# Layer 0 routing of images 0 to 2 moved into the attention loop, with its lists on GpSimd

## The chip, the cores and the metric

The kernel runs on one core of a Trainium2 chip, as one launch. Its time is the device time in microseconds (us) of that launch; the median of ten runs of the kernel before is given below. A core has five engines that run side by side, each with its own in-order queue of instructions: PE (TensorE, matrix products and transposes), ACT (ScalarE), DVE (VectorE), POOL (GpSimd) and SP (SyncE, which here issues DMAs). An instruction waits for instructions of other engines through semaphores, and while it waits, everything behind it in its own queue waits too.

## The reference, cut to what matters

The network has two layers on four images of 256 channels and 32 x 32 = 1024 tokens.

```
x  = x + attention(layernorm(x))          # layer 0, top-k attention, 8 heads, a gate sets k
t  = layernorm(x) per token, no affine    # eps 1e-5
logits = t @ router_w.T                   # 8 experts
rw, re = top_k(softmax(logits), 2); rw = rw / sum(rw)
out = t + sum over the two experts of rw * (gelu(t @ w1[e] + b1[e]) @ w2[e] + b2[e])
# layer 1: layernorm, a selective scan in four directions, layernorm,
#          and an 8-expert top-2 MoE with a per-expert layernorm and 1024 hidden columns
```

"Routing" below means all that lies between the attention's output x and the moment that the token rows stand in the expert order in DRAM: the logits, the two best experts, the mean and the deviation of each token, the two weights, the place of each token in its expert's list, and the scatter of the token rows.

## The kernel before, in words

**Attention.** A work item of the attention is a *half* (one tile of 128 queries and one group of four heads); there are 64, 16 to an image (`PER`), in the order of the images. The loop `for i in range(len(order) + 8): turn(i)` runs 72 turns. A turn works on halves of four ages at once: `h0` (this turn's half: `take` at L655 copies its scores from PSUM to SBUF on ACT, then counts begin), `h1` and `h2` (counts and updates of a threshold, L621 on ACT and L625 on DVE), and `h3` (windows and the selection on DVE, L672 and L675, then four masks on POOL, L705, and six small `verify` operations on POOL, L694 to L699). Two halves make a `Pair`, whose weights (L760, L765), exponentials (L773) and sums (L783) run in the turns after. The order in which the engines get their instructions is the order in which `turn` writes them out; nothing reorders it afterwards. The line that is run first in a turn after `h0.scores(1)` is `h0.take(0)`.

**Work beside the attention.** `plan(first, needed, steps, places)` enters a generator into a list; `beside(i, place)` takes one step of the most urgent entry at each of five places of a turn (places 0 to 4); `due` forces what is needed. So are placed the queries and keys of the next head group, the values, `rest` (the depthwise convolution, L548 to L581), and `finish` (the projection and the residual, L601 and L604), which writes the final x of image b in turns 16b + 20 to 16b + 23.

**Layer 0 routing.** Class `Routing0` handles an image in two generators. `norm` computes the logits on PE (L216), copies them on DVE, transposes the image on PE into token rows (L226), copies these on ACT (L228) into a buffer of their own (`token_rows`, one of the ring `s`), and gets the sum of squared deviations by Square on ACT (L231). `route` finds the deviation by a bit trick and three Newton steps on DVE (L256 to L261), normalises the rows on ACT (L264), picks the two experts on DVE (L270 to L281), takes the exponential for the weights on ACT (L282), counts with two matrix products (L284, L285), and places the tokens on DVE (L288 to L302). The last call also makes the table of the expert tiles. All four images are planned behind the last half: `norm` from turn 64 and turn 69 on, `route` from turn 67 and turn 70 on. After the loop, 64 indirect DMAs on POOL (L240, 16 for an image, all in one group without dependencies on each other) scatter the rows into `slots_x0`.

**Layer 0 MoE.** 36 tiles (`USUAL`) of 256 rows each; `Tile0` loads rows (L1704) and weights (L1707, L1709) on SP, transposes the rows (L1715), runs two products with a Gelu between them (L1739), multiplies by the weight on ACT (L1752), adds the residual on DVE (L1753), and stores the rows by a DMA on POOL. Behind it come the scan of layer 1 and the second MoE.

**Storage.** x of each image is a tile [128, 2, 1024] (channels in the partitions). `zeros` is a constant tile from which DMAs in turn 3 (into `slots_x`) and turn 20 (into `slots_x0`) fill two DRAM arrays.

Of the kernel before, what the change touches and what calls it, by code (L numbers as in the profile page):

```python
# [21 lines left out]
P = 128  # L22
B = 4
# [23 lines left out]
W0 = C + 3  # L47
# [15 lines left out]
def metaformer(ctx: ExitStack, tc: tile.TileContext, t: dict, out: bass.AP):  # L63
# [12 lines left out]
    x = [cons.tile([P, CT, L], F32, tag=f"x{b}", name=f"x{b}") for b in range(B)]  # L76
# [13 lines left out]
    def layer_norm_steps(dst, src, eps, room, psum, tag):  # L90

        sq = room("ln_sq")
        for h in range(NHALF):
            cols = ts(h, HALF)
            mean = psum.tile([P, HALF], F32, tag=tag, name="ln_mean")
            for c in range(CT):
                nc.tensor.matmul(mean, mean_w, src[:, c, cols], start=(c == 0), stop=(c == CT - 1))
            for c in range(CT):
                nc.vector.tensor_tensor(dst[:, c, cols], src[:, c, cols], mean, ALU.subtract)
                nc.scalar.activation(sq[:, c, cols], dst[:, c, cols], AF.Square)  # L100
# [16 lines left out]
        for h in range(NHALF):  # L117
            rb = psum.tile([P, HALF], F32, tag=tag, name="ln_rb")
            for i in range(HALF // P):
                n = h * (HALF // P) + i  # L120
                nc.tensor.matmul(rb[:, ts(i, P)], rs[:, n : n + 1].to_broadcast([P, P]), ident,
                                 start=True, stop=True)
            for c in range(CT):
                nc.vector.tensor_tensor(dst[:, c, ts(h, HALF)], dst[:, c, ts(h, HALF)], rb, ALU.mult)

    def layer_norm(dst, src, eps, pool, psum, tag):
        for _ in layer_norm_steps(dst, src, eps, lambda n: pool.tile([P, CT, L] if n == "ln_sq" else [P, NT], F32,
# [10 lines left out]
    zeros = cons.tile([P, W0], F32, tag="zeros", name="zeros")  # L138
    nc.vector.memset(zeros, 0.0)
    nc.gpsimd.iota(zeros[:, C : C + 1], [[0, 1]], base=2 * B * L, channel_multiplier=2,  # L140
                   allow_small_or_imprecise_dtypes=True)
# [11 lines left out]
    base0 = cons.tile([P, E], F32, tag="base0", name="base0")  # L153
# [10 lines left out]
    nc.gpsimd.iota(place, [[0, 1]], base=0, channel_multiplier=1, allow_small_or_imprecise_dtypes=True)  # L164
    tiles0 = cons.tile([P, PHASES, E], F32, tag="tiles0", name="tiles0")
# [23 lines left out]

    class Routing0:  # L190

        def __init__(self, space, rest, bank, group):
            self.bank, self.group, self.rest = bank, group, rest
            room = carved(space)
            self.before = room([P])
            nc.gpsimd.memset(self.before, 1.0)
            nc.gpsimd.affine_select(out=self.before, in_=self.before, pattern=[[1, P]], compare_op=ALU.is_gt,
                                    fill=0.0, base=0, channel_multiplier=-1)
            self.keep = room([E, NT])
            nc.vector.memset(self.keep, 1.0)  # L200
            nc.vector.memset(self.keep[:, :, 0:1], 0.0)
            nc.vector.tensor_copy(base0, region)
            self.small = [[room([NT]) for _ in range(2)] for _ in range(B)]
            self.logits = [room([NT, E + 1]) for _ in range(B)]

        def norm(self, b, rows, ready=(True, True)):

            ve, nm = self.small[b]
            for h in range(NHALF):
                while not ready[h]:  # L210
                    yield None
                four = slice(4 * h, 4 * h + 4)
                raw = self.bank("raw")[:, : 4 * (E + 1)].rearrange("p (n e) -> p n e", e=E + 1)
                for i in range(4):
                    for c in range(CT):
                        nc.tensor.matmul(raw[:, i], x[b][:, c, ts(4 * h + i, P)], rw0[:, c, :],  # L216
                                         start=(c == 0), stop=(c == CT - 1))
                yield True
                nc.vector.tensor_copy(self.logits[b][:, four], raw)
                nc.vector.tensor_scalar(nm[:, four], raw[:, :, E], -C ** -0.5, None, ALU.mult)  # L220
                yield False
                for r in (2 * h, 2 * h + 1):
                    tp = self.bank("tp").rearrange("p (i c) -> p i c", c=C)
                    for i in range(2):
                        for c in range(CT):
                            nc.tensor.transpose(tp[:, i, ts(c, P)], x[b][:, c, ts(2 * r + i, P)], ident)  # L226
                    yield True
                    nc.scalar.copy(rows[:, ts(r, 2), :C], tp)  # L228
                    for i in range(2):
                        n = 2 * r + i  # L230
                        nc.scalar.activation(tp[:, i], tp[:, i], AF.Square, bias=nm[:, n : n + 1], scale=C ** -0.5,  # L231
                                             accum_out=ve[:, n : n + 1])
                    yield False

        def send(self, b, rows):

            here = sent[:, :, ts(b, NT)]
            for n in range(NT):
                for k in range(2):
                    ins = nc.gpsimd.indirect_dma_start(  # L240
                        out=slots_x0, out_offset=bass.IndirectOffsetOnAxis(ap=here[:, k, n : n + 1], axis=0),
                        in_=rows[:, n], in_offset=None).ins
                    tc.declare_no_dep(ins, group=self.group, reason="rows of their own")
                    tc.add_to_no_dep_group(self.group, ins)

        def route(self, b, rows):

            here = sent[:, :, ts(b, NT)]
            room = carved(self.rest)
            wide = [P, NT, E]  # L250
            ve, nm = self.small[b]
            lg, eq, hot1, hot2, both, place_, pick = (room([NT, E]) for _ in range(7))
            tote, cum = room([E, NT]), room([E, NT])
            rr, r0, rs, red, m1, m2 = (room([NT]) for _ in range(6))
            place_ = flat(place_).rearrange("p (e n) -> p e n", n=NT)
            nc.vector.tensor_scalar(ve, ve, 1e-5, None, ALU.add)  # L256
            nc.vector.tensor_scalar(r0.bitcast(I32), ve.bitcast(I32), -0.5, RSQRT_BITS, ALU.mult, ALU.add)
            for src, dst in ((r0, rs), (rs, r0), (r0, ve)):
                nc.vector.tensor_tensor(rr, src, src, ALU.mult)
                nc.vector.scalar_tensor_tensor(rr, rr, -0.5, ve, ALU.mult, ALU.mult)  # L260
                nc.vector.scalar_tensor_tensor(dst, rr, 1.5, src, ALU.add, ALU.mult)  # L261
            nc.vector.scalar_tensor_tensor(nm, nm, C ** 0.5, ve, ALU.mult, ALU.mult)
            for n in range(NT):
                nc.scalar.activation(rows[:, n, :C], rows[:, n, :C], AF.Identity, bias=nm[:, n : n + 1],  # L264
                                     scale=ve[:, n : n + 1])
            nc.vector.tensor_tensor(lg, self.logits[b][:, :, :E], ve.unsqueeze(2).to_broadcast(wide), ALU.mult)
            yield None

            def best(value, hot):
                nc.vector.tensor_reduce(value, lg, AX.X, ALU.max)  # L270
                nc.vector.tensor_tensor(eq, lg, value.unsqueeze(2).to_broadcast(wide), ALU.is_equal)
                nc.vector.tensor_tensor(eq, eq, first.unsqueeze(1).to_broadcast(wide), ALU.mult)
                nc.vector.tensor_reduce(red, eq, AX.X, ALU.max)
                nc.vector.tensor_tensor(hot, eq, red.unsqueeze(2).to_broadcast(wide), ALU.is_equal)

            best(m1, hot1)
            nc.vector.tensor_scalar(rows[:, :, C], red, -1.0, float(E), ALU.mult, ALU.add)
            nc.vector.scalar_tensor_tensor(lg, hot1, -1e30, lg, ALU.mult, ALU.add)
            best(m2, hot2)
            nc.vector.tensor_tensor(both, hot1, hot2, ALU.add)  # L280
            nc.vector.tensor_tensor(m2, m2, m1, ALU.subtract)  # L281
            nc.scalar.activation(m2, m2, AF.Exp)  # L282
            sums = self.bank("sums")[:, : 2 * NT * E].rearrange("p (k f) -> p k f", k=2)
            nc.tensor.matmul(sums[:, 0], self.before, flat(both), start=True, stop=True)  # L284
            nc.tensor.matmul(sums[:, 1], mean_w, flat(both), start=True, stop=True)  # L285
            yield True
            sums = sums.rearrange("p k (n e) -> p k n e", e=E)
            nc.vector.tensor_scalar(tote, sums[:, 1].rearrange("p n e -> p e n"), float(C), None, ALU.mult)  # L288
# [1928 lines left out]
```

## Time and profile before

| what | us |
|---|---|
| median of 10 runs | 4078.67 |
| lowest and highest of them | 4070.32, 4088.41 |
| the profiled execution | 4079.1 |
| its span (first to last instruction) | 4077.4 |
| mean granted TensorE clock of the span | 0.877 |
| attention turns 0 to 63 | 113.6 to 1819.6 |
| turns 24, 25, 26, 27, 28 begin | 737.4, 764.9, 790.6, 818.5, 847.9 |
| first and last scatter of layer 0 (L240) | 1914.5, 1994.8 |
| first load of an expert tile (L1704) | 2002.25 |
| first transpose of the layer 0 MoE (L1715) | 2009.1 |

All times of instructions are counted from the span's start, in the one profiled execution. A row of the timeline gives the start, the duration, the engine, the line of the code, the operation, what it writes and reads, and in square brackets how long the engine had been idle before it and what ended that. In a row of the groups, the column behind the bar is busy time and the mean duration of one in nanoseconds, and then the idle time in front of the group. In the page's part 2 the span is cut into 40 slices of 102 us, and a digit is the busy share of a slice in tenths; the attention fills slices 2 to 18, and slice 20 (1937 to 2039 us) holds the scatters.

### The profile page before, as it was taken

Reading aid. Unit: us, or ns where it says so; the run is one execution under the profiler, and the core shown is the slowest. Engines: PE = TensorE matmul, PEld = TensorE weight load, DVE = VectorE, ACT = ScalarE, POOL = GpSimd, SP = SyncE. Lnnn points to the kernel's source line nnn. Section 1 sums busy time; section 2 is a strip of 40 time slices with the busy share of each in tenths; the row PEclk is TensorE's granted clock in tenths of the full one; section 3 lists DMA queues with packets and bytes.
Section 4 is the critical chain, followed back from the end, with each engine's and each line's share of the span. In section 5 each row is a group of like instructions: output and inputs, shape, how many; then the busy total and the mean of one; then the engine's idle time right before and its main releaser. Section 6 shows DMA issues by size and latency. Waiting matters only on the chain. (4 is left out here: it accounts for less than half of the span.)

```text
span 4077.4 us, 50231 instructions
## 1 busy us (share of the span) xinstructions
PE 3519.6 (86%) x17474; PEld 1951.2 (48%) x17474; DVE 3022.7 (74%) x5391; ACT 2833.8 (70%) x3793; POOL 1786.8 (44%) x1437
## 2 busy tenths in 40 slices
PE   8378888788788878877498999999999999999996
PEld 5134434434343434334275434444444434788885
DVE  2689898989998898896366899899899899411112
ACT  2889999999999998995135666767767677422222
POOL 0145444554554444655434656445445446121111
PEclk8567788788878877787699999999999999999997
DMA  9400094000000000000475434334324334655565
GB/s 288 101 1 1 1 237 111 1 1 19 1 1 1 11 1 1 1 11 22 144 227 163 117 107 133 104 100 126 116 97 127 108 103 139 192 184 187 187 193 191
DMA packets 241817, 393.34 MB, mean 96 GB/s; under 512 B 31888, under 2 KB 182160, under 8 KB 241424
## 3 DMA queue, kind: packets, MB, share of 16 engines
q1 hardware_dynamic: 218992, 340.51, 27.9%
q0 software_dynamic: 19904, 48.42, 3.6%
q8 instruction: 141, 2.31, 0.2%
q10 hardware_dynamic: 2656, 1.09, 0.1%
q14 instruction: 124, 1.02, 0.1%
HBM read 280.34 MB, written 109.61 MB: 96 GB/s over the span
## 5 line engine op out<-in xcount | busy, mean ns | idle before, releaser
L705 POOL TENSOR_SCALAR dr<-s_n,last 128x1024 bf16<-128x1024 f32 x256 | 731.4, 2875 | 881.2 <-DVE state L733 425.6
L621 ACT ACTIVATE junk_a<-s_n,state 128x1024 int8<-128x1024 f32 x448 | 514.5, 1149 | 25.1 <-DVE state L739 6.9
L1889 POOL TENSOR_TENSOR da_c<-prod,come 128x1024 f32<-128x1024 f32 x128 | 247.7, 1935 | 436.1 <-DVE h L1895 385.5
L625 DVE TENSOR_SCALAR_CACHE_REDUCE junk_v<-s_n,state 128x1024 int8<-128x1024 f32 x320 | 408.6, 1277 | 8.8
L2065 ACT ACTIVATE hid<-hp,b 128x256 f32<-128x256 f32 x288 | 133.7, 474 | 355.5 <-PE hp L2063 355.3
L672 DVE SCALAR_TENSOR_TENSOR w<-s_n,win 128x1024 f32<-128x1024 f32 x256 | 347.4, 1357 | 5.3
L675 DVE MAX8 win<-w 128x8 f32<-128x1024 f32 x256 | 314.5, 1228 | 8.8
L1856 POOL TENSOR_TENSOR uu<-dx,bb 128x1024 f32<-128x1024 f32 x127 | 302.3, 2381 | 1.6 <-DMA bb<-bc_d 1.6
L621 ACT ACTIVATE junk_a<-s_n,guess 128x1024 int8<-128x1024 f32 x256 | 294.0, 1149 | 7.4
L773 ACT ACTIVATE ex<-sT 128x1024 f32<-128x1024 f32 x256 | 247.0, 1015 | 66.0 <-PE sT L765 65.8
L1895 DVE TENSOR_TENSOR_SCAN h<-da_c,uu 128x1024 f32<-128x1024 f32 x127 | 288.6, 2272 | 0.0
L1869 DVE TENSOR_TENSOR_SCAN h<-da,uu 128x1024 f32<-128x1024 f32 x127 | 288.4, 2271 | 0.0
L1878 DVE TENSOR_TENSOR_SCAN h<-da,uu 128x1024 f32<-128x1024 f32 x127 | 287.3, 2262 | 0.0
L783 PE MATMUL o_ps<-ex,vT 128*32 128x256 f32 x2048 | 240.2, 455 | 39.2 <-ACT ex L773 32.7
L655 ACT COPY s_n<-sp 128x1024 f32<-128x1024 f32 x256 | 256.7, 1003 | 23.3 <-PE sp L647 10.8
L1840 ACT ACTIVATE da_c<-delta,a_log 128x1024 f32<-128x1024 f32 x128 | 268.6, 2098 | 5.9 <-issue 5.8
L1899 PE MATMUL hp<-h,ident 128*128 128x512 f32 x512 | 250.8, 613 | 22.8 <-DVE h L1895 22.6
L2063 PE MATMUL hp<-xe,w 128*128 128x256 f32 x1152 | 258.6, 381 | 6.3 <-DVE xe L2051 6.1
L2074 DVE TENSOR_TENSOR ys<-yp,b2e 128x512 f32<-128x512 f32 x36 | 24.9, 692 | 320.2 <-PE yp L2071 320.2
L2071 PE MATMUL yp<-w2e,hid 128*128 128x256 f32 x1152 | 255.9, 379 | 0.0
L1864 PE MATMUL hp<-da_c,ident 128*128 128x512 f32 x512 | 248.0, 607 | 6.4 <-POOL da_c L1889 3.7
L1857 ACT COPY uu<-uu 128x1024 f32<-128x1024 f32 x127 | 252.0, 1985 | 1.7 <-POOL uu L1856 1.7
(598 smaller groups left out, 7438.3 us busy)
## 6 DMA issues: line engine op xcount, KB each, us to landing
cb<-bc_d SPq DMA_DIRECT2D x128, 512.0 KB, 4.1
bb<-bc_d SPq DMA_DIRECT2D x127, 512.0 KB, 5.0
w<-in_w SPq DMA_DIRECT2D x36, 1024.0 KB, 5.3
w2e<-in_w SPq DMA_DIRECT2D x36, 1024.0 KB, 5.6
slots_x<-zeros SPq DMA_DIRECT2D x1, 33411.0 KB, 133.9
slots_x<-zeros SPq DMA_DIRECT2D x1, 33282.0 KB, 129.4
w<-in_w SPq DMA_DIRECT2D x72, 256.0 KB, 3.4
xs<-slots_x SPq DMA_DIRECT2D x36, 259.0 KB, 3.5
```

Source lines behind the costliest of these rows:

```text
L621: nc.scalar.activation(junk, self.row(r), AF.Sign, bias=thr, scale=-1.0, accum_out=u)
L625: nc.vector.tensor_scalar(junk, self.row(r), thr, None, ALU.is_lt, ALU.add, accum_out=u)
L655: nc.scalar.copy(self.s[e][:, :, ts(h, HALF)], self.sp[h][e])
L672: nc.vector.scalar_tensor_tensor(w, self.row(r), self.win[:, r, 0:1], self.row(r), ALU.is_gt if r < LAST_DVE else ALU.is_ge, ALU.subtract, ...
L675: nc.vector.max(out=self.win[:, r, 1:], in_=w)
L705: ins = nc.gpsimd.tensor_scalar(dr, self.row(r), self.last[:, r : r + 1], None, ALU.is_lt)
L1840: nc.scalar.activation(grid(self.da_c), cols_flipped(self.prep.delta[:, self.c]), AF.Exp, scale=self.decay)
L1856: nc.gpsimd.tensor_tensor(self.uu[:, 0], self.prep.dx[:, self.c], self.bb, ALU.mult)
L1869: nc.vector.tensor_tensor_scan(rows.rearrange("p r w -> p (r w)"), self.da, self.uu[:, 0], 0.0, ALU.mult, ALU.add)
L1878: nc.vector.tensor_tensor_scan(hs[:, ::-1], self.da[:, ::-1], self.uu[:, 0][:, ::-1], 0.0, ALU.mult, ALU.add)
L1895: nc.vector.tensor_tensor_scan(hs, self.da_c, self.uu[:, 1], 0.0, ALU.mult, ALU.add)
L2063: nc.tensor.matmul(hp[:, f % 2], self.w1[:, c, ts(f, P)], self.xe[:, c], start=(c == 0), stop=(c == CT - 1))
```

## The change

- x is kept in a wider tile `store` of 8 rows of `W0` = 261 columns; while layer 0 runs, it is read as `xr[b][:, n, :]`, 128 tokens n by 256 channels, with five spare columns (before three). `block(b, c, h)` is the view that the layer norm, queries and keys, values, `rest` and `finish` use in place of the slice of x.
- For images 0 to 2 the routing is planned in the attention itself, from turn0 = 16b + 24 on (24, 40 and 56). `feed` (PE logits, DVE choice of two experts, transposes on PE, ACT copies into x's own place) is planned from place 0 of turn0 - 1; `count` from place 3 of turn0 + 1.
- The deviation is computed on POOL, in the new calls `behind_masks`, which stand behind the masks and `verify` of the turn: `spread` for tiles 0 to 3 in turn0 + 1, `spread` for tiles 4 to 7 and `root` in turn0 + 2; `locate` in turn0 + 3; and two scatters in each of the turns turn0 + 5 to turn0 + 12, now not in a group without dependencies.
- The exponential of the weights is in `share`, called by `before_masks` right behind `h0.take(0)` of turn0 + 3. `shares` (two operations on DVE) is in turn0 + 3, `fix` (DVE) in turn0 + 4.
- Image 3 is routed in two halves (`halved`), planned from turns 68 and 70; its 16 scatters follow the loop. `table` is a function of its own.
- Rows are scattered as they are, not normalised. `Tile0.normed` normalises them on ACT (two activations of 128 x 256 for a tile) before the transposes; `small` gets two more DVE operations, and in `store` the multiplication is an activation with a bias of the same size.
- The two DMA fills change places (turn 3 and turn 20); the ring `s` is sized 2 x 1024 again; the second layer's residual operation on DVE that added op to x becomes a copy; `before` and `bases` are shared by the layers.

The core of the diff:

```diff
+        for b in range(B - 1):
+            turn0 = b * PER + 24
+            routings[turn0] = Routing0(b, bank, lambda: scratch("space0"))
+            plan((turn0 - 1) * PLACES, turn0 + 1, routings[turn0].feed())
+            plan((turn0 + 1) * PLACES + 3, turn0 + 3, routings[turn0].count())
+
+        def behind_masks(i):
+            for turn0, routing in routings.items():
+                at = i - turn0
+                if at == 1:
+                    routing.spread((0, 1))
+                if at == 2:
+                    routing.spread((2, 3))
+                    routing.root()
+                if at == 3:
+                    routing.shares()
+                    routing.locate()
+                if at == 4:
+                    routing.fix()
+                if 5 <= at < 13:
+                    send(routing.b, (at - 5,), None)
+
+        def before_masks(i):
+            for turn0, routing in routings.items():
+                if i - turn0 == 3:
+                    routing.share()
...
             if h0:
                 h0.scores(1)
                 h0.take(0)
+            before_masks(i)
             beside(i, 0)
...
                 h3.verify()
...
+            behind_masks(i)
             beside(i, 3)
```

The new POOL work and the exponential:

```diff
+        def spread(self, pairs):
+            for r in pairs:
+                nc.gpsimd.tensor_tensor(self.squares, xr[self.b][:, ts(r, 2), :C],
+                                        self.mean[:, ts(r, 2)].unsqueeze(2).to_broadcast([P, 2, C]), ALU.subtract)
+                nc.gpsimd.tensor_tensor(self.squares, self.squares, self.squares, ALU.mult)
+                half = C // 2
+                while half > 1:
+                    nc.gpsimd.tensor_tensor(self.squares[:, :, :half], self.squares[:, :, :half],
+                                            self.squares[:, :, half : 2 * half], ALU.add)
+                    half //= 2
+                nc.gpsimd.tensor_tensor(self.ve[:, ts(r, 2)], self.squares[:, :, 0], self.squares[:, :, 1], ALU.add)
+
+        def root(self):
+            nc.gpsimd.tensor_scalar(self.ve, self.ve, 1.0 / C, 1e-5, ALU.mult, ALU.add)
+            nc.gpsimd.tensor_tensor(self.rs, self.ve, minus_half, ALU.pow)
+            nc.gpsimd.tensor_tensor(self.rr, self.rs, self.rs, ALU.mult)
+            nc.gpsimd.tensor_tensor(self.rr, self.rr, self.ve, ALU.mult)
+            nc.gpsimd.tensor_scalar(self.rr, self.rr, -0.5, 1.5, ALU.mult, ALU.add)
+            rs, shift = xr[self.b][:, :, C + 4], xr[self.b][:, :, C + 3]
+            nc.gpsimd.tensor_tensor(rs, self.rs, self.rr, ALU.mult)
+            nc.gpsimd.tensor_tensor(self.m2, self.m2, rs, ALU.mult)
+            nc.gpsimd.tensor_tensor(shift, self.mean, rs, ALU.mult)
+            nc.gpsimd.tensor_scalar(shift, shift, -1.0, None, ALU.mult)
+            nc.gpsimd.tensor_scalar(xr[self.b][:, :, C], self.code, 1.0, None, ALU.mult)
+
+        def share(self):
+            nc.scalar.activation(self.m2, self.m2, AF.Exp)
```

The other steps of the three images, cut to their operations:

```diff
+        def feed(self):
...
+            for n in range(NT):
+                for c in range(CT):
+                    nc.tensor.matmul(raw[:, n], xr[b][:, n, ts(c, P)], rw0[:, c, :], start=(c == 0), stop=(c == CT - 1))
+            yield True
+            self.chosen_two(raw)
+            yield False
+            for r in range(NT // 2):
+                tp = self.bank("tp").rearrange("p (i c) -> p i c", c=C)
+                for i in range(2):
+                    for c in range(CT):
+                        nc.tensor.transpose(tp[:, i, ts(c, P)], xr[b][:, 2 * r + i, ts(c, P)], ident)
+                yield True
+                nc.scalar.copy(xr[b][:, ts(r, 2), :C], tp)
+                yield False
...
+        for h in range(NHALF):
+            plan((68 + 2 * h) * PLACES, 100 + h, last_image(h))
...
-        for b in range(B):
-            routing[0].send(b, token_rows[b])
+        for h in range(NHALF):
+            send(B - 1, range(4 * h, 4 * h + 4), "scatter0")
...
+            def normed(self):
+                self.xn = pb.tile([P, T // P, C], F32, tag="xn", name="xn")
+                for a in range(T // P):
+                    nc.scalar.activation(self.xn[:, a], self.xs[:, a, :C], AF.Identity,
+                                         bias=self.xs[:, a, C + 3 : C + 4], scale=self.xs[:, a, C + 4 : C + 5])
...
-            for step in ("load", "small", "turned", "hidden", "result", "store"):
+            for step in ("load", "normed", "small", "turned", "hidden", "result", "store"):
```

## The prediction

> **What bounds the kernel now.** I read the page's busy shares and slices first, for the stages; then the turns one by one in the table by stretches and the timeline, for what each engine does in them; then the end of the attention in the timeline.
>
> ```profile
> PE   8378888788788878877498999999999999999996
> DVE  2689898989998898896366899899899899411112
> ACT  2889999999999998995135666767767677422222
> POOL 0145444554554444655434656445445446121111
> ```
>
> In slices 3 to 18 (the attention) ACT is at 9 and DVE at 8 to 9, and POOL at 4 to 6. From 113.6 to 1794.8 us, 63 turns, ACT is busy 1571.4 of 1681.2 us: a turn is 26.7 us, of which ACT idles 1.74. So the attention is bound by ACT with DVE close behind, and a microsecond that ACT has to wait is nearly a microsecond of the kernel. Slice 20 is nearly empty: the hole that the change is about.
>
> ```profile
> 1914.49 1.25 POOL L240 DMA_INDIRECT slots_x<-token_rows,sent  x1 [19.98 <-issue]
> 1916.04 0.98 POOL L240 DMA_INDIRECT slots_x<-token_rows,sent  x1 [0.30 <-issue]
> ...
> 1994.78 0.96 POOL L240 DMA_INDIRECT slots_x<-token_rows,sent  x1 [0.30 <-issue]
> 2002.25 0.40 SPq L1704 DMA_DIRECT2D xs<-slots_x  x1
> ...
> 2009.13 1.09 PE L1715 MATMUL tp<-ident,xs 128*128 128x128 f32 x4 [29.45 <-DVEq L1759]
> ```
>
> 64 scatters at 1.27 us (0.96 and an idle 0.30) take POOL from 1914.5 to 1995.7; the last has landed at 2002.25, 6.5 us later, and then the MoE's first load goes out. PE idles 29.45 us.
>
> **Part 1: what the tail gives back.** Turn 64 begins at 1819.6. (a) Before, three images are routed between the last turns. The last masks of the attention end at 1892.8, and the four quarters of weights, exponentials and sums behind them, each 5.6 us by its rows (L760 1.15, L765 1.07, L773 1.91, L783 1.48), last until 1934.9 instead of 22 us, because logits, transposes, rows (L264, 4.03 us of ACT for an image) and lists stand between them. The last norm ends at 1937.1. After, POOL reaches the last masks some 7 us sooner (DVE waited 9.84 us at 1860 for logits that are no longer there; image 2's scatters, still on POOL in turns 64 to 68, take part of it back): masks end near 1886, the four quarters near 1908, and the first half of image 3 (PE 4, ACT 4.2 and DVE 3.6 in a row, partly hidden) puts 7 between them; last norm 1918. (b) Behind it came finish, image 3, the table and the rest of 64 scatters, 1937.1 to 2002.25. Now: finish 6, the second half's routing 17 (PE 4, ACT and DVE 4, count 2, then 30-odd DVE operations of 0.17 to 0.22, 6.5), 8 scatters 10, landing 6.5: about 1958. **Gain 44 us.** Bounds: 36, if image 3's first half and the scatters on POOL cost 4 each more; 52, if they hide.
>
> **Part 2: the wait that the change puts on ACT.** Its place is turn 27 (and 43, 59), where `share` stands right behind `take(0)`. In the order of ACT's instructions the Exp comes directly behind the first two copies, and it waits for POOL: for `m2` times the deviation, the seventh operation of `root`. `root` stands on POOL behind turn 26's masks, its `verify`, and the second `spread`. Where those are in the profile:
>
> ```profile
> 810.29 11.31 POOL L705 TENSOR_SCALAR dr<-s_n,last 128x1024 bf16<-128x1024 f32 x4 [16.10 <-DVE junk_v L625]
> ...
> 822.94 0.26 POOL L699 TENSOR_TENSOR fine<-fine,sure 128x36 f32<-128x36 f32 x1
> ```
> ```profile
> 818.46 2.04 ACT L655 COPY s_n<-sp 128x1024 f32<-128x1024 f32 x2
> 820.53 1.15 ACT L621 ACTIVATE junk_a<-s_n,guess 128x1024 int8<-128x1024 f32 x1
> ```
>
> Turn 27 begins at 818.46, so ACT is at the Exp at 820.5. At that time turn 26's masks still run; they end at 821.6, and `verify` at 823.2. Only then do the 20 operations of `spread` begin. The profile has no such sequence, but POOL's prices by size:
>
> ```profile
> L1856 POOL TENSOR_TENSOR uu<-dx,bb 128x1024 f32<-128x1024 f32 x127 | 302.3, 2381 | 1.6 <-DMA bb<-bc_d 1.6
> L1889 POOL TENSOR_TENSOR da_c<-prod,come 128x1024 f32<-128x1024 f32 x128 | 247.7, 1935 | 436.1 <-DVE h L1895 385.5 <-PE y L1906 50.6
> L694 POOL TENSOR_TENSOR sure<-win 128x32 f32<-128x32 f32 x64 | 16.0, 250 | 0.0
> L1000 POOL TENSOR_TENSOR yy<-yy,half 128x1 f32<-128x1 f32 x1 | 0.6, 578 | 105.2 <-DVE half L999 105.2
> ```
>
> Between 32 columns (0.25) and 1024 (2.38, or 1.94 with a broadcast operand) lie 512 at 1.27 and 1.08, 256 at 0.73, 128 at 0.46, 64 at 0.32, then 0.25, 0.23 and three at 0.21 (the row of 128x4, L695, is 0.22). The ten operations of a pair are 4.97, and as each needs the one before (in `verify` a dependent operation starts 0.07 to 0.10 later), 5.7 with the gaps; two pairs 11.4. Seven operations of `root` at 0.21 to 0.25 and a power of 0.7 (0.58 is the row for one column; eight times it, 4.6, is the upper end), 2.5 with gaps. So the Exp can start at 823.2 + 11.4 + 2.5 = 837.1, and **ACT waits 16.6 us**, with the counts, copies and exponentials of turn 27 queued behind it; DVE and PE run dry behind those. Turn 43 and turn 59 have masks that end 3.4 and 3.6 us after their start (3.1 in turn 27): 16.9 and 17.1. Sum 50.6. What comes back: ACT idles 3.80 at 836 to 839.8 for PE's weights (L765), but that chain begins with ACT's own L581 in the same turn, so it moves along; I take 1 us a turn, so 47.5. Bounds: 36, if the small operations cost nothing and half of ACT's idle of the next two turns returns; 62, with the dear power and POOL stretched.
>
> **Part 3: the same work inside full turns.** For an image: ACT 4 copies of 0.59, one of 72 columns at 0.35, the Exp 0.20: 3.0 us; DVE some 20 operations of 0.17 to 0.22: 4.6; PE 11 to 12 (logits 3.9, transposes 2.6 to 4.4, counts 4). PE idles 3 to 7 us in each of turns 24 to 28 and hides its share. ACT's idle in these five turns is 10.4 us and DVE's 17.2, so nothing at the lower end; all of both, 8, at the upper, as they wait in turn for each other. I take 5, so **15 us** for three. POOL before its next masks: turn 25's masks and `verify` end at 794.3, `spread` of two pairs at 806, and masks come at 810.3: covered by 4 us.
>
> The trace also has a cost of POOL beside DVE: L672, a DVE operation with two inputs, takes 1.28 us with no mask beside it (137 of them) and 1.52 under one (114); L625, with one input, does not change (1.27 and 1.28). Four L672 a turn in the two turns of `spread` are at most 1.9 us an image, inside the 5. The Trainium skill ("GPSIMD Engine Reference", Specifications) says that GpSimd shares its SBUF interfaces with VectorE and contends with DVE instructions of two SBUF inputs; it speaks against this place for the work. It gives no price there; if the two simply took turns, POOL's `spread` would lengthen by the four L672 in it, 5 us, and the three waits by 15, where the row gives the small stretch.
>
> **Part 4: the MoE and the rest.** `normed` adds 2 x 0.587 (the row of L264) to ACT in front of the transposes. From 2010 to 2180 PE is busy 147.8 of 170 us, ACT 70.5, DVE 108.7; with 4.5 us a tile ACT goes from 1.9 to 3.1. PE's products hide it, save the 1.2 in front of the first tile; I take **+2**. Bounds: 0, and 18 if in each tile 0.5 of it stands between load and transposes. Two DVE operations of 0.2 a tile, the exchanged fills, the views with a stride and the copy in place of an addition (0.69 before) I cost at nothing: DVE has a third of the MoE free, and the fills move between turns of which none waits for a DMA.
>
> **Sum**, against the profiled execution of 4079.1 (the median 4078.67 is 0.4 below): -44 + 47.5 + 15 + 2 = +20.5, so 4099 us.
>
> **Rivals.**
> (1) *Faster: ACT's wait is made up.* One mechanism: behind the wait PE and POOL stand ahead, and the turns after run at ACT's own 25 us instead of 26.7 until the lead is used. At 1.7 us a turn, ten turns return it all; the wait then costs 3 to 7 an image: -44 + 15 + 10 + 2, 4062 us. It decides below 6 us an image. For it: PE is busy 80% at a granted clock of 0.78. Against it: ACT's idle is mostly a chain between PE's single bank and ACT inside one turn, which a lead does not shorten. 0.22.
> (2) *Nearly even*: tail at 52, waits at 45, turns at 5 to 8: 4079. 0.13.
> (3) *Worse: gain lost elsewhere too.* The dear power and stretched `spread` (20 an image), 8 an image in the turns, and 10 to 18 in the MoE, where ACT's in-order queue couples `normed` to the Gelu of the tile before: 4125 to 4140. 0.15.
> (4) *The change doesn't do what it says*: `feed` finds its places taken by `rest` and comes only when it is due; then POOL waits for its means in front of the masks, and the time is that of (3). Within its chance.
>
> My forecast has 0.50. Slower by over 0.2% (8 us, about what a measurement can tell from none) 0.65, within 0.13, faster 0.22. The range takes in the upper bounds without the last of (3), and most of (1): 4052 to 4138.
>
> **What would show it.** In the new profile: an Exp on 128 x 8 early in turns 27, 43 and 59 with 14 to 20 us of ACT's idle in front of it, released by POOL; POOL's `spread` at 5.5 to 6 us a pair; the last scatter near 1950 plus what the attention lost, and the first load 7 us behind it; no ACT wait of note in the MoE's tiles. I am wrong if the Exp finds POOL done, if the turns after it are shorter than before, or if the hole between the last norm and the first load is not shortened by over 20 us.

## The result, and the profile after

The changed kernel takes 4110.78 us (median of 8 runs, 4106.66 to 4113.03) beside 4077.45 before (28 runs): a ratio of 1.0082, interval 1.0073 to 1.0091. It is slower by 33 us, 0.8%, on the chip of these runs; on two other chips, below, the kernel before is itself about 40 us slower, and on the one of them where both were timed the kernel after is faster by 0.2%. The profiled execution after took 4110.56, its span is 4108.9 (before 4079.1 and 4077.4).

The busy shares by slice, of the kernel after:

```profile
PE   8378878878887978785687999999999999999996
DVE  2788898979997898968466899899899899411112
ACT  2989999979997998885356667667667677422222
POOL 0146454665557554756233655445445446221111
```

ACT has a seven now in slices 9 and 13 and an eight in 17 and 18, where before all four were nines; POOL has more fives, sixes and sevens. In slices 9, 13 and 18 lie the turns in which ACT waits. The timeline of ACT at the start of turn 27:

```profile
819.29 1.91 ACT L764 COPY s_n<-sp 128x1024 f32<-128x1024 f32 x2
840.06 0.21 ACT L321 ACTIVATE space<-space 128x8 f32<-128x8 f32 x1 [18.87 <-POOL space L308]
```

L321 is the Exp of `share`, L308 the seventh operation of `root`. The three Exps wait 57.0 us together. What POOL did in that time, from its timeline (822.4 is the end of turn 26's masks, 824.0 that of `verify`):

```profile
824.00 1.04 POOL L290 TENSOR_TENSOR space<-x,space 128x512 f32<-128x512 f32 x1
...
830.57 1.90 POOL L292 TENSOR_TENSOR space<-space 128x512 f32<-128x512 f32 x1
832.55 3.71 POOL L295 TENSOR_TENSOR space<-space 128x256 f32<-128x256 f32 x7
...
836.91 1.69 POOL L302 TENSOR_TENSOR space<-space,minus_half 128x8 f32<-128x8 f32 x1
...
839.82 0.21 POOL L308 TENSOR_TENSOR space<-space,x 128x8 f32<-128x8 f32 x1
```

The second `spread` takes 12.6 us and `root` 3.4 to its seventh operation; the power alone takes 1.69. The end of the tail, in the timeline after:

```profile
2009.63 0.96 POOL L212 DMA_INDIRECT slots_x<-x,sent  x1 [0.30 <-issue]
...
2022.06 0.40 SPq L1836 DMA_DIRECT2D xs<-slots_x  x1
...
2026.99 1.13 PE L1853 MATMUL tp<-ident,xn 128*128 128x128 f32 x4 [20.71 <-ACT xn L1846]
```

Against the kernel before, stage by stage. A turn's length is from the first ACT copy of its scores to that of the next turn, in the two profiled executions:

| stage | before | after | difference | forecast |
|---|---|---|---|---|
| lead-in, up to turn 0 | 113.6 | 109.3 | -4.2 | 0 |
| turns 27, 43, 59 | 86.9 | 141.1 | +54.2 | +47.5 |
| the other turns up to the start of turn 63 | 1594.4 | 1608.4 | +14.0 | +15 |
| start of turn 63 to the first load of an expert tile | 207.4 | 163.2 | -44.2 | -44 |
| first load to first transpose | 6.9 | 4.9 | -1.9 | with the MoE |
| first to last transpose of the layer 0 MoE | 204.0 | 215.6 | +11.6 | +2 |
| the rest | 1864.2 | 1866.3 | +2.1 | 0 |
| span | 4077.4 | 4108.9 | +31.5 | +20.5 |

### The profile page after: what moved, and what is told of

Its sections match the earlier page's. It is cut to its first block, busy times and chain, and to the rows that moved or that the text cites. A ratio compares the mean times of both kernels' runs of the same rounds, so it can differ in the third digit from the quotient of the medians.

```text
span 4108.9 us, 50486 instructions
## 1 busy us (share of the span) xinstructions
PE 3523.4 (86%) x17586; PEld 1967.6 (48%) x17586; DVE 3041.5 (74%) x5408; ACT 2840.2 (69%) x3798; POOL 1874.0 (46%) x1621
## 5 line engine op out<-in xcount | busy, mean ns | idle before, releaser
L781 DVE SCALAR_TENSOR_TENSOR w<-s_n,win 128x1024 f32<-128x1024 f32 x256 | 354.3, 1384 | 5.5
L764 ACT COPY s_n<-sp 128x1024 f32<-128x1024 f32 x256 | 245.6, 1003 | 23.5 <-PE sp L756 17.5
L2218 POOL DMA_INDIRECT results<-ys,to x72 | 70.0, 972 | 405.6 <-DVE ys L2216 179.4
```

The source lines that it names most:

```text
L781: nc.vector.scalar_tensor_tensor(w, self.row(r), self.win[:, r, 0:1], self.row(r), ALU.is_gt if r < LAST_DVE else ALU.is_ge, ALU.subtract, ...
```

## The experiments

The twelve runs went in three groups of four, each group on one chip, and the chips differ: the kernel before took 4079.74 beside the first group, 4116.47 beside the second and 4119.27 beside the third. So ratios hold inside a group, and between groups only stages of the profiles are compared. "First chip" below is that of the first group; the runs of the result, with 4077.45 for the kernel before, are counted with it, though it is not known that they had the same chip.

**First group. e1_later:** the Exp and what follows it one turn later.

```diff
-                if at == 3:
+                if at == 4:
                     routing.shares()
                     routing.locate()
-                if at == 4:
+                if at == 5:
                     routing.fix()
-                if 5 <= at < 13:
-                    send(routing.b, (at - 5,), None)
+                if 6 <= at < 14:
+                    send(routing.b, (at - 6,), None)
...
-                if i - turn0 == 3:
+                if i - turn0 == 4:
                     routing.share()
```

> Exp, shares and locate, fix and the scatters each one turn later (turns 28, 44, 60 for the Exp). Theory A (the change loses by ACT's wait for POOL at the Exp, 57.0 us in the three turns, and nothing brings it back): the three waits go, turns 27, 43 and 59 are again 28 to 30 us instead of 46 to 47, and the time is 4111 - 57 = 4054 us (4048 to 4062), faster than before by 0.4 to 0.7%. Theory B (ACT's wait only takes the place of other waits, of DVE and PE in the same turns): part of it comes back as other idle time, 4075 to 4100. Theory C (the Exp waits for something else than the length of POOL's queue): it waits in turn 28 as well, 4100 and more.

Measured 4061.26 (7 runs), a ratio to before of 0.9967 (0.9955 to 0.9979): inside Theory A's 4048 to 4062, at its upper end, faster than before by a little less than A's 0.4 to 0.7%, and far from B and C. In ACT's timeline the Exp stands behind its copies without a wait:

```profile
845.40 1.01 ACT L764 COPY s_n<-sp 128x1024 f32<-128x1024 f32 x1 [0.80 <-PE sp L756]
846.31 0.21 ACT L321 ACTIVATE space<-space 128x8 f32<-128x8 f32 x1
```

Turns 27, 43 and 59 are 28.78, 28.75 and 28.77 us (29.42, 28.72, 28.72 before). The other turns keep what they cost: from turn 20 to turn 63 the attention is 17.5 us longer than in the profile before, 5.6 of it in turn 23, 4.9 in turn 39 and 4.2 in turn 37. Not all of this is the change's: e3, whose attention is that of the kernel before, has turn 37 longer by 3.9 and turn 39 by 2.0 as well. Tail and MoE are as in the kernel after (162.2 from turn 63 to the first load, 215.0 for the tiles).

**e2_twice:** the second `spread` is run twice.

```diff
                     routing.spread((2, 3))
+                    routing.spread((2, 3))
                     routing.root()
```

> The kernel after with the second spread (tiles 4 to 7) done twice in turns 26, 42 and 58: 20 more POOL operations in front of root, 12 to 13 us an image by the profile after. Theory A: ACT's wait grows from 19 to 31 an image one for one, the time by 36 to 39, to about 4148. Theory B: the engines behind have slack, growth by less than half, below 4130. Theory C: no growth, 4111.

One execution: 4129.01. The time alone, 18 us over the kernel after, misses Theory A's 4148 and lies in Theory B's range below 4130; the profile speaks for A. The wait in front of the Exp, in ACT's timeline:

```profile
838.82 0.21 ACT L321 ACTIVATE space<-space 128x8 f32<-128x8 f32 x1 [30.07 <-POOL space L308]
```

The three waits are 89.2 us, 32.2 more than in the kernel after, and turns 27, 43 and 59 are 10.8, 10.2 and 10.8 longer than there: one for one. In this execution turn 20, which lies ahead of all that the edit touches, began 11 us sooner than in the profile after, and that hides a third of it. So in the turns Theory A holds and B and C fall: the wait is POOL's queue in front of `root`, and a microsecond more in it is a microsecond of the turn. That it is one of the whole kernel rests on this one execution's stages, not on its time.

**e3_moe_copy:** the kernel before with two copies on ACT in front of the transposes.

```diff
+            def normed(self):
+                self.xn = pb.tile([P, T // P, C], F32, tag="xn", name="xn")
+                for a in range(T // P):
+                    nc.scalar.activation(self.xn[:, a], self.xs[:, a, :C], AF.Identity)
...
-                        nc.tensor.transpose(tp[:, c, ts(a, P)], self.xs[:, a, ts(c, P)], ident)
+                        nc.tensor.transpose(tp[:, c, ts(a, P)], self.xn[:, a, ts(c, P)], ident)
```

> The kernel before with two ACT copies (Identity, no scale and bias) of 128 x 256 put in front of the transposes of each tile of the layer 0 MoE, and nothing else. If ACT's in-order queue couples them to the Gelu (profile after: tiles at 3.2, 5.1 and 5.8 us in turn, mean 4.70, where before had 4.35): +9 to +13 us, about 4089. If the extra 11.6 us of the MoE came from the two new DVE operations or the row's layout: 0 to +3, about 4079.

Measured 4085.49 (11 runs), 1.0022 (1.0010 to 1.0034): +5.7, between the two. The tiles in the middle stay at 4.3 us, where the kernel after has 3.2, 5.1 and 5.8 in turn; first to last transpose 207.4. The copies cost, but they do not make the pattern of the kernel after. e8 and e9 go on from here.

**e4_later_pool:** e1_later with the rows normalised on POOL.

```diff
-                    nc.scalar.activation(self.xn[:, a], self.xs[:, a, :C], AF.Identity,
-                                         bias=self.xs[:, a, C + 3 : C + 4], scale=self.xs[:, a, C + 4 : C + 5])
+                    nc.gpsimd.tensor_scalar(self.xn[:, a], self.xs[:, a, :C], self.xs[:, a, C + 4 : C + 5],
+                                            self.xs[:, a, C + 3 : C + 4], ALU.mult, ALU.add)
```

> e1_later with the rows of the layer 0 MoE normalised on POOL (a multiplication and an addition with two columns, 128 x 256) instead of ACT. If ACT's queue is what slows the MoE: tiles back near 4.35 to 4.45 us, 8 to 11 less than e1_later, about 4044. If POOL's operations (about 0.9 each) or their meeting DVE's two-input operations take as much: the same as e1_later or up to 10 more.

Measured 4074.90 (11 runs), 0.9989 (0.9978 to 1.0000): 13.6 slower than e1_later, beyond what either case had. Both were half right: up to tile 18 the tiles run at 4.3 each, and then one takes 25.2 us, as the operation (0.78) stands in POOL's queue behind 16 gathers for the next layer of 0.94 to 1.64. First to last transpose is 231.5; up to the transposes of the 22nd tile it is 115.3 against 101.2 in e1_later, 14.1 of the 16.5 us that the stage is longer. A later tile takes 29.8, but without a gather in front of it; e7 below, which has no row on POOL, has 27.3 at that place.

**Second group. e5_same_turn:** the kernel after with one line moved.

```diff
-            before_masks(i)
             beside(i, 0)
...
                 h3.verify()
...
+            before_masks(i)
             behind_masks(i)
```

> The kernel after with one edit: the Exp stays in turns 27, 43 and 59 but its call stands behind the selection and the masks' issue instead of behind the first copies, so ACT reaches it some 17 us later in the turn, when root is done within 1 to 4 us. Theory A (what matters is how early in ACT's order the Exp stands): ACT's wait in front of it falls from 19 to 4 at most, and where it stays, it lies in the 3.8 us that ACT idled there before the change; time 4055 to 4068, as e1_later (4061) or up to 4 less, since image 2's scatters come a turn sooner. Theory B (any wait for POOL in that turn costs it in full): 4075 and more.

Measured 4060.05 (4 runs), 0.9853 of the kernel before on this chip. The waits of the three Exps fall from 57.0 to 7.8 us, the longest of them in turn 43:

```profile
1284.47 0.21 ACT L321 ACTIVATE space<-space 128x8 f32<-128x8 f32 x1 [3.19 <-POOL space L308]
```

Turns 27, 43 and 59 are 28.8, 29.9 and 29.2. Theory A again: the price was the place in ACT's order, not the work. The scatters' coming a turn sooner gave nothing that can be seen: turn 63 to the last scatter is 155 us, in e1_later 152.

**e6_mix and e7_dve:** e1_later with other engines for the rows.

```diff
+                    if self.i < 18:
+                        nc.gpsimd.tensor_scalar(self.xn[:, a], self.xs[:, a, :C], self.xs[:, a, C + 4 : C + 5],
+                                                self.xs[:, a, C + 3 : C + 4], ALU.mult, ALU.add)
+                    else:
+                        nc.scalar.activation(self.xn[:, a], self.xs[:, a, :C], AF.Identity,
...
```

> e1_later with the rows of the first 18 expert tiles normalised on POOL, those of the other 18 on ACT. In e4 the tiles on POOL ran at 4.3 each until POOL's gathers for the next layer began, and then at up to 30. If that is the whole reason of e4: the first 18 tiles at 4.3 instead of 4.7, the others as in e1_later: 5 to 7 less than e1_later, about 4055. If POOL's work delays the gathers anyway: 4061 and more.

> e1_later with the rows of all expert tiles normalised on DVE (two operations of 128 x 256 with two columns as scalars). DVE was busy 3.4 of 4.35 us a tile, so if they take 0.3 to 0.4 each there is room: tiles at 4.35 to 4.5, 5 to 10 less than e1_later, 4051 to 4056. If DVE's in-order queue couples as ACT's did: 4061 or more.

e7 has the same operation as e4 with `nc.vector` for `nc.gpsimd`, for all tiles. e6 measured 4053.40 (4 runs), e7 4050.96 (5 runs, 0.9837, interval 0.9817 to 0.9858). As e1_later was not in this group, the stages are compared: first to last transpose 213.6 for e6 and 211.5 for e7 against 215.0. The tiles in the middle are at 4.3 in both. The gain of e6 in this stage is smaller than expected, and its later tiles fall back to ACT's 3.2, 5.1 and 5.8; in e7 the DVE operation takes 0.425 and the tiles stay at 4.3. Both times lie near or inside what was expected, but as the chip is another than e1_later's, the times alone show no gain over it. e7 has the lowest median of the study; it was not timed on the first chip.

**e8_moe_all and, in the third group, e9_moe_pointers:** the kernel before with the whole MoE part of the change, in neutral values.

e8 adds to e3's edit (`nought` is a tile of zeros, `ones` in e9 one of ones):

```diff
+                self.shift = pb.tile([P, T // P], F32, tag="shift", name="shift")
+                nc.vector.tensor_tensor(self.shift, self.best, nought, ALU.mult)
+                nc.vector.scalar_tensor_tensor(self.best, nought, 1.0, self.best, ALU.add, ALU.mult)
...
-                    nc.scalar.mul(self.ys[:, a], self.ys[:, a], self.wt[:, a : a + 1])
+                    nc.scalar.activation(self.ys[:, a], self.ys[:, a], AF.Identity, bias=self.shift[:, a : a + 1],
+                                         scale=self.wt[:, a : a + 1])
```

And e9 to e8's:

```diff
-                    nc.scalar.activation(self.xn[:, a], self.xs[:, a, :C], AF.Identity)
+                    nc.scalar.activation(self.xn[:, a], self.xs[:, a, :C], AF.Identity,
+                                         bias=nought[:, a : a + 1], scale=ones[:, a : a + 1])
```

> The kernel before with the whole MoE part of the change in neutral values: the two ACT operations of e3_moe_copy, two DVE operations of 128 x 2 more, and the multiplication in front of the store as an activation with a bias of zeros. e3 measured +5.7 for the ACT operations alone, the profile after shows +11.6 in the MoE. If the three small additions upset the order of ACT (tiles of 3.2, 5.1, 5.8 in turn): +10 to +14, about 4091. If the rest of the 11.6 comes from elsewhere (the start of the stage, the branch): +5 to +7, about 4086.

> e8_moe_all with one thing more: the two ACT operations in front of the transposes take a scale and a bias from columns (ones and zeros), as in the kernel after. In the profiles such an operation takes 0.589 us, without columns 0.404 (e3, e8), and e8's tiles ran at 4.3 in the middle of the stage where after has 3.2, 5.1, 5.8. If ACT's time per tile is what tips the order (2 x 0.19 more): the middle tiles at 4.6 to 4.8 in the mean, the MoE 4 to 8 longer than e8's between first and last transposes. If not: 4.3, and the slow tiles of the change come from its other data.

e8 measured 4120.95 (12 runs), 1.0009 (0.9995 to 1.0023), which is +4.5, and its middle tiles stay at 4.3; the expected +10 to +14 did not come. e9 measured 4129.08 (12 runs), 1.0029 (1.0016 to 1.0042), which is +9.8, and its middle tiles show 3.2, 5.1, 5.8, a mean of 4.7, as the kernel after does. First to last transpose is 217.1 in e8 and 219.9 in e9, 2.8 longer where 4 to 8 were expected; the second half of the stage differs between executions (below). The groups by line of 45 us, some ten tiles, of the stage, first of e3, then of e8, of e9 and of the kernel after:

```profile
L1714 ACT ACTIVATE xn<-xs 128x256 f32<-128x256 f32 x20 | 8.0, 404 | 0.0
```
```profile
L1763 ACT ACTIVATE ys<-ys,shift,wt 128x256 f32<-128x256 f32 x18 | 9.7, 589 | 1.5 <-DVE ys L1759 1.5
```
```profile
L1719 ACT ACTIVATE xn<-xs,nought,ones 128x256 f32<-128x256 f32 x19 | 10.6, 589 | 0.0
L1766 ACT ACTIVATE ys<-ys,shift,wt 128x256 f32<-128x256 f32 x20 | 10.9, 592 | 8.6 <-DVE ys L1762 8.6
```
```profile
L1846 ACT ACTIVATE xn<-xs 128x256 f32<-128x256 f32 x20 | 11.1, 589 | 0.0
L1893 ACT ACTIVATE ys<-ys,shift,wt 128x256 f32<-128x256 f32 x20 | 10.9, 592 | 10.1 <-DVE ys L1889 10.1
```

The same operation takes 0.404 us without columns and 0.589 with them. With 0.37 us more a tile in ACT's queue the wait of the rows' multiplication (`ys`) for DVE grows from 1.5 us in e8 to 8.6 to 10.1 in some ten tiles, and the next Gelu stands behind that wait.

**Third group. e10_before16:** the kernel before without the scatters of images 0 to 2.

```diff
-        for b in range(B):
+        for b in range(B - 1, B):
             routing[0].send(b, token_rows[b])
```

> The kernel before with the scatters of images 0 to 2 left out (48 of 64; their rows stay zero, so the MoE and what follows work on other data, and only the times up to the first expert tile are read). If POOL's queue of 64 scatters decides the end of the tail, the first load comes 30 us sooner, as image 3's lists are ready near 1965. If the routing of images 0 to 2 between the last turns is what the tail loses by, image 3's rows are ready no sooner than before (1974, table 1980) and the first load comes only 5 to 10 us sooner, near 1993 to 1998.

One execution, of which only the tail is read. The first load is at 2001.7, as in the profile before on the first chip (2002.25), where at least 5 us less were expected: with 64 scatters POOL's queue ends there at 1995.7, and here with 16 at 1996.7, since image 3's own rows are ready only at 1976. In the profile before POOL is through with the 48 other scatters at about 1975 (1914.5 and 48 times 1.27), so there their queue held up image 3 by next to nothing; then what the tail gave back is the routing of images 0 to 2 between the last turns and the routing of image 3 in halves. For the first chip this is argued from a run on the third, and not shown.

On the other chips it is not so. e8 and e9, with all 64 scatters and the attention of the kernel before, have their last scatter end at 2028.9 and 2031.1, 33 to 35 us later than the first chip's 1995.7, though turn 63 begins 2 to 4 us sooner than there. On the third chip the first load is at 2036.4 in e9 and at 2001.7 in e10: 35 us go with the scatters of images 0 to 2, in one execution each. Three rows of e8's timeline, then two of e10's:

```profile
1966.96 0.20 DVE L219 COPY kept<-raw 128x36 f32<-128x36 f32 x1 [16.08 <-issue]
1967.37 3.75 PE L601 MATMUL pp<-att,wproj 128*128 128x512 f32 x4 [14.48 <-issue]
...
1983.14 0.59 ACT L228 COPY token_rows<-tp 128x512 f32<-128x512 f32 x1 [38.40 <-remote]
```
```profile
1950.35 0.59 ACT L228 COPY token_rows<-tp 128x512 f32<-128x512 f32 x1 [13.64 <-PE tp L226]
...
1976.38 1.25 POOL L240 DMA_INDIRECT slots_x<-token_rows,sent  x1 [80.71 <-issue]
```

In e8 the DVE copy stands for 14 us after its input from PE is there (at 1952.9), and the products of L601, which in the profile before wait for this copy, start right behind it. ACT's 38.40 is for the most part a wait for transposes that come late behind this (1977.5 to 1978.6); 4.5 us of it have no reason in the program. In e10, on the chip of e9, the same ACT copy waits 13.64 us, all of it for PE, and the DVE copy starts as soon as PE is done. So with the scatters in flight DVE, and ACT for a shorter time, stand without a reason that the profile shows.

A guess is that they wait for their code. The Trainium skill ("Runtime: NRT & Kernel Launch", Instruction fetch mechanics) says that each engine refills its instruction memory in blocks through a DMA queue of its own while it runs, and takes it as mostly hidden. No run here shows that the waits are such refills. Between 1910 and 1985 us the DMA queues that carry instructions moved 9 packets in the profile before and in e10, and 3 in e8; but a program that runs 30 us late also fetches late, and in e8 none of these packets moves between 1915 and 1978.6, while DVE goes on at 1966.96, which speaks against the guess for that wait. What holds the engines, and why only on some chips, stays open.

**e11_shift:** e7_dve with `turn0 = b * PER + 25`.

> e7_dve (Exp one turn later, rows normalised on DVE, 4051 us) with all routing of images 0 to 2 one turn later still (turn0 = 16b + 25). In all profiles after, turns 23 and 39 are 5 us longer than before, where feed's logits and transposes meet finish in the same bank. If that meeting costs it: 8 to 12 less in the three images, part of it lost again in the tail to image 2's later scatters, about 4045. If feed costs the same wherever it stands: the 5 us move to turns 24 and 40, about 4051 to 4056.

Measured 4062.67 (5 runs, 4050.03 to 4066.84), above what either case had. Turn 23 is as before (26.72 against 26.70), and turn 24 is 2.9 longer; turn 39 is 1.0 and turn 40 2.9 longer. Against e7, turns 23, 39 and 55 are 5.1, 3.9 and 4.7 shorter and turns 24, 40 and 56 are 4.2, 3.8 and 3.7 longer: nearly all of the cost moved with `feed`, as the second case had it, and the meeting with `finish` is worth 1 us an image at most. From turn 20 to turn 63 the attention is 24 us longer than before, against 12.5 in e7; the difference lies in the turns behind an image's `feed` (7.3 in turns 27 to 35, 6.2 in turns 43 to 51), where the lists and scatters now stand a turn later, and why they cost more there is not tested. Nothing is gained.

**e12_after:** the kernel after, unchanged, on the third chip.

> The kernel after, unchanged, beside the kernel before on whatever chip this group gets: on the chip of e5 to e8 the kernel before took 4116 instead of 4078 and the kernels with the scatters inside the attention did not, so the worth of the change may differ by chip. On a chip like the first: ratio 1.006 to 1.010. On one like the second: 0.995 to 1.000.

Measured 4110.51 (10 runs) beside 4119.27: 0.9981 (0.9966 to 0.9997). The kernel after takes the same as on the first chip (4110.78); it is the kernel before that is 40 us slower on this one. Its waits are the same too (57.8 us in the three Exps).

## Why the prediction came out as it did

The forecast was slower by 20.5 us and 4099; measured are 4110.8, inside the range of 4052 to 4138, with the sign and the mechanism of the likeliest case.

- **The wait on ACT (part 2)**: right in place, cause and releaser, shown by e1, e2 and e5. Mis-sized in the term: 47.5 forecast, 54.2 measured. Masks and `verify` ended 3.1 and 4.7 us into turn 27, as taken from before. The second `spread` was 12.6 instead of 11.4: its first pair took 5.4, less than the 5.7 forecast, and its second 7.1, because two DVE operations (L781) each held POOL up by 0.85 (below). So the two engines took turns, a case that the prediction had priced at 5 us and left out of its sum; but two such operations met this `spread`, not four, and cost 1.7. The power took 1.69 instead of 0.7, and the waits were 19.0 in the mean instead of 16.9. Of them 1 us a turn was taken to come back, and in the three turns themselves 0.9 did (57.0 against 54.2); in the turns just behind turn 27 some 3 more came back, in e12 about 1, behind turn 59 nothing.
- **The tail (part 1)**: -44.2 against -44. Its steps held as well: the last norm ends at 1981.9, and 1918 plus the 64 that the attention lost is 1982. Two errors cancel: the second half's routing took 14 and not 17, and the first load came 11.5 us behind the last scatter and not 6.5, as the table ends at 2007.5 and the branch and the small loads behind it now stand in the open.
- **Full turns (part 3)**: +14.0 against +15, and 17.5 in e1. That it agrees to 1 us is luck: from turn 20 to turn 63 kernels with the attention of before take 1165.5 (e9) to 1175.9 (e10), and 1169.0 in the profile before. What stands out in every kernel with the change's timing is turn 23, 39 and 55, 5.6, 5.6 and 3.1 longer in the profile after, where ACT waited 4.45, 4.05 and 3.94 us for the first transposes of `feed`; the cost was not spread over five turns. POOL's cover in turn 26 was 1.0 us where 4 was taken, but it held. The first of these waits:

```profile
729.15 0.59 ACT L257 COPY x<-tp 128x512 f32<-128x512 f32 x1 [4.45 <-PE tp L255]
```

- **The MoE (part 4)**: the step that failed. "PE's products hide it, save the 1.2 in front of the first tile" gave +2; first to last transpose is +11.6, and by the medians the MoE part of the change costs 9.8 (e9 against its own before). In the middle of the stage they are not hidden: from the 4th to the 21st tile it takes 80.1 us after and 74.7 before. ACT had time (36 of 60 us busy), but its order had not: e9 shows that two operations of 0.589 are enough to turn its slack into waits for DVE. But that pattern is not where the profile's 11.6 stand. The stage in two stretches, up to the 22nd tile's transposes and behind them, before and then after (behind each stretch its length, the busy time and count of PE, weight loads, DVE, ACT and POOL, the granted clock, and the DMA):

```profile
2009.10:2108.40 99.30, 89.39 (x409) 72.10 (x410) 65.29 (x210) 35.46 (x79) 23.23 (x26) 0.93 0.73 223
2108.40:2213.10 104.70, 88.88 (x393) 65.90 (x392) 70.96 (x180) 47.10 (x82) 45.85 (x41) 0.92 0.63 175
```
```profile
2027.00:2126.20 99.20, 89.33 (x415) 71.64 (x416) 66.66 (x232) 61.34 (x127) 25.48 (x28) 0.97 0.80 234
2126.20:2242.60 116.40, 93.45 (x388) 67.84 (x387) 74.22 (x206) 66.66 (x110) 45.82 (x39) 0.88 0.54 152
```

  The first stretch is even, as its first three tiles take 7.0 us less after; all of the difference is in the second, where the tiles share the engines with the first work of layer 1. There PE is busy 4.6 us longer at a lower granted clock, and stands 7 us more. e8, without the pattern, takes 118.0 us for that stretch and e9, with it, 110.8. So the cost and its size are shown, and ACT's order is shown as the cause in the middle tiles; what makes up the second stretch stays open. The upper bound of 18 held.
- **Lead-in**: 4.2 shorter, unforeseen. Its first two stretches of 20 us have a granted clock of 0.96 and 0.87 after and 0.89 and 0.86 before, and in the other profiles turn 20 begins up to 11 us sooner than in the profile after; single executions differ there, and the change has no part in it that is shown.
- **Rivals**: (1) fell: the turns behind the wait do not win it back, only taking the Exp out of POOL's way does (e1, e5). (3) has its MoE term, 10 to 18, and its wait of 20 an image is nearer the measured 19.0 than the forecast's 16.9; it does not have its 8 an image in the turns. (4) did not occur.

## What to carry to other kernels

Before a small operation is put early into the queue of the engine that bounds a stage, follow its input back through the other engine's queue to the time when that engine starts on it; here one activation of 0.2 us cost 18 us an image, and moving its call down the turn or into the next made the kernel faster than the one before (on the first chip by 0.3%). An engine with 40% of its time free could here not take more work at no cost, as it feeds a tight chain in order: look for the wait that is shortest now, not for the busy share. A forecast of one stage that agrees to 1 us means little where executions of the same code differ by 10. And as the kernel before took 40 us more on two chips of three, with its scatters beside the routing, time such a kernel on more than one chip.

## What the runs showed of the hardware

POOL and DVE shut each other out. In turn 27 of the kernel after, a DVE operation of 128 x 8 with two inputs met POOL's first `spread` operation (824.00 to 825.04, shown above):

```profile
824.12 0.93 DVE L839 SCALAR_TENSOR_TENSOR fr<-bracket,aim,dd 128x8 f32<-128x8 f32 x1
```

It takes 0.23 elsewhere and here ends when POOL's ends. The reverse stands above too: L292 at 830.57 took 1.90 instead of 1.05, beside a DVE L781 that ended at 831.57. In the whole profile after, 25 DVE operations with two tensor inputs start inside one of POOL's longer `spread` operations (0.3 us and more): the 18 small ones end 0.02 to 0.05 us behind POOL's, the 7 of 128 x 1024 1.08 us behind it, and none of the 28 other DVE operations that start there is lengthened by more than 0.1. The Trainium skill ("GPSIMD Engine Reference", Specifications) names the contention with DVE instructions of two SBUF inputs; the trace agrees, and adds that in these rows the one that comes second stands until the other instruction has ended.

An ACT Identity of 128 x 256 costs 0.404 us without a scale and bias from columns and 0.589 with them. The power on POOL costs 1.69 us for 128 x 8 and 0.58 for 128 x 1, while a multiplication of 128 x 8 costs 0.20.
